# A quantized gated FFN issued from a list plan, with one elementwise step of its sigmoid on GpSimd

## The chip, the cores and the metric

The kernel runs on one core of a Trainium2 chip. The metric is the device time of one execution in microseconds; the number quoted for a kernel is the median of its runs. Five engines matter, each with its own queue, worked through in order: TensorE (PE in the profile, with PEld for its weight loads), VectorE (DVE), ScalarE (ACT), GpSimd (POOL) and SyncE (SP, which issues DMAs here). An instruction that waits for another engine holds up everything behind it in its own queue.

## The reference, cut to what matters

The reference is a two-layer decoder in float32 on x of 16 x 256 tokens with 256 features: in layer 0 a causal linear attention, a cross-attention and a mixture of experts, in layer 1 a latent attention, a second cross-attention and a gated FFN with simulated 16-bit activations. The change touches only this last FFN:

```python
def act_qdq(x):
    qmax = 2.0 ** (ACT_BITS - 1) - 1.0                      # 32767
    scale = jnp.maximum(jnp.max(jnp.abs(x)) / qmax, 1e-12)  # over the whole tensor
    return jnp.clip(jnp.round(x / scale), -qmax - 1.0, qmax) * scale
def fixed_qdq_u16(x):
    scale = 1.0 / 65536.0
    return jnp.clip(jnp.round(x / scale), 0.0, 65535.0) * scale
...
x = act_qdq(x)
up = act_qdq(x @ lpbq_dequant(w_up).T)
gate = act_qdq(x @ lpbq_dequant(w_gate).T)
sig = fixed_qdq_u16(jax.nn.sigmoid(gate))
gate = act_qdq(gate * sig)
o = act_qdq(gate * up)
return o @ lpbq_dequant(w_down).T
```

There are 4096 tokens, 256 features and 768 inner features. Each scale is a maximum over a whole tensor, so nothing can be rounded before the last element of that tensor is known. Each act_qdq is a barrier.

## The kernel before, in words

The FFN is the function l1_ffn, the last stage. Tokens lie along the free dimension in 8 groups of 512 (index n); the normalised input of a group, transposed, is F.xT[n] (tile ff_x). The 768 inner features are worked in 3 parts of 256 (index c), so that there are 24 *pieces* (n, c), each a tile of 128 partitions x 1024 floats. G[n] (ff_g) holds the gate branch of a group for the whole stage. The stage has four passes:

1. Gate. The input is rounded (rounded, L1746, on ScalarE; L1773 on VectorE) and multiplied with the gate weights; ScalarE copies each product out of PSUM (L1776), VectorE takes its peak (helper peak, L1681). Ends with scales(): a maximum over the peaks (L1732, VectorE), an all-reduce over partitions (L1734, GpSimd), a scale (L1737) and its reciprocal (L1739) on VectorE.
2. Up, first time, and the sigmoid. For each piece TensorE makes the up product, of which only the peak is kept (ff_pu). At the same time, independently of TensorE, the gate piece is rounded (ScalarE, tile ff_a), goes through the sigmoid (L1790, ScalarE, tile ff_b), is clamped to 65535/65536 and shifted by 192 (L1793), so that the low half of each float holds the 16-bit value, and is multiplied with the rounded gate (L1794, VectorE); then its peak is taken (ff_ps). Ends with two scales.
3. Up again. The same up product is made a second time, rounded straight from PSUM (ff_a), multiplied with the rounded gate (L1809) and its peak taken (ff_po). Ends with a scale.
4. Down. Each piece is rounded (L1746, L1818) and multiplied with the down weights; each output tile of 128 tokens (32 of them) is scaled and added to x (L1826) and written by a DMA from SP (L1827).

Tiles: ff_a and ff_b have three buffers each, shared by passes 2 and 3; gate and up products share three PSUM buffers (pu[...]), the output has two (po). TensorE can thus be three pieces ahead of whoever reads PSUM. A float32 matmul call appears as two matmul records. Matmuls are issued by the helper matmul_k (L422).

The order on each engine: the stages before l1_ffn run under planned(E), where E.nc is a Plan. A Plan only records calls, and Plan.issue then schedules the list: it finds what each call reads and writes, gives each a cost on its engine (class Call: VectorE 50 + 1.05 ns an element, ScalarE activation 170 + 0.73, GpSimd tensor_scalar 50 + 1.2, TensorE 0.84 twice), and picks again and again, on each engine, the call of lowest rank (place in the program) among those that could start within 150 ns of the earliest:

```python
first = min(rows)[0]
rank, index, begin, n = min(
    (r, i, b, n) for b, r, i, n in rows if b <= first + self.near
)
```

Ring objects tell the plan when a buffer of a tile ring comes free. The finished order is issued as it stands, sorted by planned start (`with self.tc.manual_schedule()`). Calls issued from a plan carry the line L322 in the profile. The FFN before is not in a plan: its calls go straight to the engines in program order and the framework's own scheduler settles each engine's order, which is why its profile lines are its own.

Of the kernel before, what the change touches and what calls it, by code (L numbers as in the profile page):

```python
# [22 lines left out]
ALU = mybir.AluOpType  # L23
AX = mybir.AxisListType
PSUM = bass.MemoryType.PSUM
# [301 lines left out]
@contextmanager  # L327
def planned(E):

    nc = E.nc  # L330
    E.nc = plan = Plan(E.tc)
    yield plan
    E.nc = nc
    plan.issue()
# [1345 lines left out]
def peak(E, out, in_, axis=AX.X):  # L1680
    E.nc.vector.tensor_reduce(out, in_, axis, ALU.max, apply_absolute_value=True)  # L1681
# [25 lines left out]
def l1_ffn(E, F):  # L1707
# [5 lines left out]

    tc, nc = E.tc, E.nc
    I16, U16 = mybir.dt.int16, mybir.dt.uint16
    MC = 2
    NP = MI // MC
    with ExitStack() as ctx:  # L1720
        c1 = ctx.enter_context(tc.tile_pool(name="ff_c", bufs=1))
        big = ctx.enter_context(tc.tile_pool(name="ff_g", bufs=1))
        wk = ctx.enter_context(tc.tile_pool(name="ff_w", bufs=3))
        pu = ctx.enter_context(tc.tile_pool(name="ff_pu", bufs=3, space=PSUM))
        po = ctx.enter_context(tc.tile_pool(name="ff_po", bufs=2, space=PSUM))
        up, gate, down = (E.ffn[n] for n in ("up", "gate", "down"))

        def scales(peaks, name, unit=None):
# [15 lines left out]
        def rounded(out, in_, inv):  # L1744

            nc.scalar.activation(out, in_, AF.Identity, bias=F.magic[:, 0:1], scale=inv[:, 0:1])  # L1746

        def low16(t, dtype):
            return t.bitcast(dtype)[:, :, ::2]
# [3 lines left out]
        def branch(w, n, c, name):  # L1753

            ps = pu.tile([P, MC, 512], F32, name="ps_" + name, tag="pu")
            for m in range(MC):
                f = slice((c * MC + m) * P, (c * MC + m + 1) * P)
                matmul_k(
                    E, ps[:, m, :], [w[:, k, f] for k in range(KD)],
                    [F.xT[n][:, k, :] for k in range(KD)],  # L1760
                )
            return ps

        def piece(n, c):
            return G[n][:, c * MC : (c + 1) * MC, :]
# [17 lines left out]
        for at, (n, c) in enumerate(pieces):  # L1783
            ps = branch(up, n, c, "up")
            peak(E, stat["u"][:, at : at + 1], ps, AX.XY)
            gp = piece(n, c)
            gq = wk.tile([P, MC, 512], F32, name="ff_a", tag="ff_a")
            rounded(gq, gp, ig)
            sig = wk.tile([P, MC, 512], F32, name="ff_b", tag="ff_b")
            nc.scalar.activation(sig, low16(gq, I16), AF.Sigmoid, scale=sg[:, 0:1])  # L1790


            nc.vector.tensor_scalar(sig, sig, 65535.0 / 65536.0, 192.0, ALU.min, ALU.add)  # L1793
            nc.vector.scalar_tensor_tensor(  # L1794
                gp, low16(gq, I16), sg16, low16(sig, U16), ALU.mult, ALU.mult
            )
            peak(E, stat["s"][:, at : at + 1], gp, AX.XY)
# [60 lines left out]
@with_exitstack  # L1858
def tile_decoder(ctx: ExitStack, tc: tile.TileContext, ins: dict, out: bass.AP):
    E = make_env(ctx, tc, ins, out)  # L1860
    with ExitStack() as outer:
        made = outer.enter_context(tc.tile_pool(name="weights_1", bufs=1))
        with ExitStack() as inner:
            W = load_weights(E, outer, inner)
            l0_attention(E, W)
            raw = load_weights_1(E, inner.enter_context(tc.tile_pool(name="raw_1", bufs=1)))
            routed, V = l0_cross(E, W, raw, made)
        with ExitStack() as inner:

            fw = ffn_weights(E, ctx, inner)  # L1870
            W.moe = inner.enter_context(tc.tile_pool(name="moe_weights", bufs=2))
            psum = inner.enter_context(tc.tile_pool(name="made_ps", bufs=1, space=PSUM))
            steps = {1: "gate", 3: "up", 5: "down"}
            l0_experts(
                E, W, routed, lambda e: fw(steps[e], psum, "pp") if e in steps else None
            )
        F = ffn_input(E, ctx)
        l1_tokens(E, W, F, V, routed)
    l1_ffn(E, F)
# [45 lines left out]
```

## Time and profile before

| what | us |
|---|---|
| median of 3 runs (1784.87 to 1789.61) | 1785.4 |
| the profiled execution | 1783.88 |
| its span, first to last instruction | 1782.1 |
| PE busy in the span | 1634.5 (92%) |
| DVE busy | 1131.0 (63%) |
| ACT busy | 697.9 (39%) |
| POOL busy | 502.9 (28%) |
| FFN: first gate matmul to the end of the span | 1422.9 to 1782.1 |

Busy times are of the whole program; they say which engine has most work, not which sets the pace of a stage. A group line of the profile reads: line, engine, operation, output<-inputs, shapes, count, then busy time in us, mean ns of one, and the idle time of the engine just before, with what ended it. A timeline line reads: start in us from the span's start, length in us, engine, line, operation. Lengths of neighbouring VectorE instructions overlap a little, so the pace of an engine is read from starts.

### The profile page before, as it was taken

How to read it: one execution, taken by the hardware profiler on the slowest of the kernel's cores; microseconds unless marked ns; L12 is line 12 of the kernel's file. 1: busy time of each engine (PE TensorE's matmuls, PEld its weight loads, DVE VectorE, ACT ScalarE, POOL GpSimd, SP SyncE). 2: the span in 40 equal slices, each digit the busy share in tenths (PEclk: the TensorE clock that was granted, in tenths of full speed). 3: DMA queues.
4: the chain of work that ended last, by engine and by line, in shares of the span. 5: the costliest groups of instructions: out<-in, count | busy, mean ns of one | idle time of the engine just before them, and what ended most of it. 6: DMA issues, size and time to landing. Idle time of an engine off the chain costs nothing.

```text
span 1782.1 us, 24580 instructions
## 1 busy us (share of the span) xinstructions
PE 1634.5 (92%) x9428; PEld 1077.5 (60%) x9428; DVE 1131.0 (63%) x2290; ACT 697.9 (39%) x1467; POOL 502.9 (28%) x547
## 2 busy tenths in 40 slices
PE   5999997999999769999997799999999599989899
PEld 3666664666666557777776466666666344434388
DVE  7867667998888633221212789876767543998751
ACT  2223222655555311111111455465556233656650
POOL 6333213455556420000001776534334100000000
PEclk9999998999999769999999899999999699999999
DMA  5000007210111133343341111000000000000011
GB/s 174 1 1 1 1 1 241 66 32 28 34 34 37 57 131 118 108 147 119 107 133 50 51 57 36 28 1 1 1 1 1 1 0 0 1 0 0 0 45 50
DMA packets 73375, 84.48 MB, mean 47 GB/s; under 512 B 11614, under 2 KB 64566, under 8 KB 73258
## 3 DMA queue, kind: packets, MB, share of 16 engines
q1 hardware_dynamic: 67114, 66.35, 11.7%
q0 software_dynamic: 6144, 16.57, 2.9%
q8 instruction: 74, 1.21, 0.3%
q14 instruction: 43, 0.35, 0.1%
HBM read 49.56 MB, written 33.56 MB: 47 GB/s over the span
## 4 chain that ended last, share of the span: by engine, by line
PE 66%; DVE 21%; issue 7%; ACT 3%; POOL 2%; DMA 1%; SPq 0%; POOLq 0%; DVEq 0%; ACTq 0%
PE ps_h L422 8%; PE ps_y L422 8%; PE ps_pr L322 7%; PE ps_av L322 7%; PE ps_sc L322 6%; PE ps_gate L422 5%; PE ps_out L422 5%; PE ps_pt L322 4%; PE ps_v L322 3%; PE ps_rec L322 3%; PE ps_po L322 3%; DVE x L322 2%; DVE ff_g L1794 2%; DVE ff_ps L1681 2%; PE ps_ht L322 1%
## 5 line engine op out<-in xcount | busy, mean ns | idle before, releaser
L1558 DVE COPY ex_y<-ps_y 128x256 f32<-128x256 f32 x80 | 34.0, 424 | 231.3 <-PE ps_y L422 231.3
L422 PE MATMUL ps_up<-ff_x,ffn_up 128*128 128x512 f32 x384 | 167.6, 595 | 10.6 <-DVE ff_pu L1681 7.8
L322 POOL DMA_INDIRECT ex_yg<-moe_y,slot x64 | 63.2, 988 | 341.6 <-DMA moe_y<-ex_y 321.2
L322 POOL TENSOR_TENSOR sa_e<-sa_e,sa_rec 128x1024 f32<-128x1024 f32 x64 | 121.4, 1904 | 118.0 <-PE ps_pt L322 62.7
L322 ACT ACTIVATE sa_e<-ps_sc,sa_top 128x256 f32<-128x256 f32 x256 | 118.4, 485 | 69.1 <-DVE sa_top L322 65.0
L422 PE MATMUL ps_h<-ex_xT,w 128*128 128x320 f32 x512 | 142.8, 437 | 0.0
L422 PE MATMUL ps_y<-w,ex_h 128*128 128x256 f32 x640 | 140.7, 379 | 0.0
L422 PEld LDWEIGHTS ps_up<-ff_x,ffn_up 128*128 128x128 f32 x384 | 72.1, 190 | 105.9 <-issue 83.0
L422 PEld LDWEIGHTS ps_y<-w,ex_h 128*128 128x128 f32 x640 | 121.6, 190 | 18.2
L1548 ACT ACTIVATE ex_h<-ps_h 128x640 f32<-128x640 f32 x64 | 45.1, 704 | 221.3 <-PE ps_h L422 221.3
L422 PEld LDWEIGHTS ps_h<-ex_xT,w 128*128 128x128 f32 x512 | 96.7, 191 | 40.0 <-issue 0.6
L322 POOL TENSOR_TENSOR lx_s<-lx_s,lx_mx 128x616 f32<-128x616 f32 x64 | 77.5, 1224 | 51.6 <-DVE lx_mx L322 35.1
L422 PE MATMUL ps_out<-ffn_down,ff_g 128*128 128x256 f32 x384 | 85.3, 386 | 7.3 <-issue 7.3
L422 PE MATMUL ps_gate<-ff_x,ffn_gate 128*128 128x512 f32 x192 | 85.4, 608 | 6.4 <-DVE ff_x L1773 6.4
L422 PEld LDWEIGHTS ps_out<-ffn_down,ff_g 128*128 128x128 f32 x384 | 74.4, 194 | 18.7 <-issue 8.1
L322 ACT COPY lx_sT<-ps_pt 77x512 f32<-77x512 f32 x117 | 65.4, 581 | 49.8 <-PE ps_pt L322 49.4
L322 DVE TENSOR_TENSOR la_at<-ps_sc,la_tri 128x1024 f32<-128x1024 f32 x64 | 76.0, 1217 | 13.9 <-PE ps_sc L322 13.9
L322 PE MATMUL ps_pt<-ident,lx_s 128*77 128x128 f32 x512 | 77.0, 285 | 6.4 <-DVE rt_hits L322 3.7
L322 DVE TENSOR_REDUCE sa_top<-ps_sc 128x4 f32<-128x1024 f32 x64 | 75.9, 1214 | 10.7 <-PE ps_sc L322 10.7
L322 PE MATMUL ps_ht<-ident,h 128*128 128x128 f32 x256 | 38.8, 293 | 42.1 <-DVE h L322 24.8
L322 PEld LDWEIGHTS ps_pt<-ident,lx_s 128*77 128x77 f32 x512 | 58.7, 150 | 25.4 <-issue 10.7
L322 POOL DMA_INDIRECT moe_x<-rh,slot x64 | 63.5, 992 | 27.7 <-issue 10.1
(295 smaller groups left out, 3419.4 us busy)
## 6 DMA issues: line engine op xcount, KB each, us to landing
w<-in_L_ffn_w SPq DMA_DIRECT2D x32, 512.0 KB, 4.4
moe_x<-rt_zero SPq DMA_DIRECT2D x16, 640.0 KB, 7.6
ex_xg<-moe_x SPq DMA_DIRECT2D x16, 640.0 KB, 6.9
moe_y<-ex_y SPq DMA_DIRECT2D x16, 640.0 KB, 5.9
x<-in_x SPq DMA_DIRECT2D x32, 128.0 KB, 3.2
out_x<-x SPq DMA_DIRECT2D x32, 128.0 KB, 1.7
w_ctx_T<-in_ctx_T SPq DMA_DIRECT2D x1, 1232.0 KB
lx_bias<-in_mask_Bx1xSxS_ff SPq DMA_DIRECT2D x8, 154.0 KB, 2.4
```

Source lines behind the costliest of these rows:

```text
L322: made = getattr(getattr(self.nc, self.engine), self.method)(*self.args, **self.kwargs)
L422: E.nc.tensor.matmul(ps, a, b, start=n == 0, stop=n == last)
L1548: nc.scalar.activation(h[:, f, :].rearrange("p (a c) -> p a c", a=2), ps[:, :, :HC], AF.Gelu)
L1558: nc.vector.tensor_copy(y[:, c, :], ps)
L1681: E.nc.vector.tensor_reduce(out, in_, axis, ALU.max, apply_absolute_value=True)
L1794: nc.vector.scalar_tensor_tensor(gp, low16(gq, I16), sg16, low16(sig, U16), ALU.mult, ALU.mult)
```

## The change

The FFN's calls are recorded in a Plan and issued from it, with Ring objects for the pools of three and two buffers, and the clamp and shift of the sigmoid goes to GpSimd in place of VectorE. The arithmetic, the tiles, their buffer counts and the number of instructions stay.

```diff
-    tc, nc = E.tc, E.nc
+    tc = E.tc
...
-    with ExitStack() as ctx:
+    with ExitStack() as ctx, planned(E) as nc:
         c1 = ctx.enter_context(tc.tile_pool(name="ff_c", bufs=1))
         big = ctx.enter_context(tc.tile_pool(name="ff_g", bufs=1))
-        wk = ctx.enter_context(tc.tile_pool(name="ff_w", bufs=3))
-        pu = ctx.enter_context(tc.tile_pool(name="ff_pu", bufs=3, space=PSUM))
-        po = ctx.enter_context(tc.tile_pool(name="ff_po", bufs=2, space=PSUM))
+        wk = nc.ring(ctx.enter_context(tc.tile_pool(name="ff_w", bufs=3)), 3)
+        pu = nc.ring(ctx.enter_context(tc.tile_pool(name="ff_pu", bufs=3, space=PSUM)), 3)
+        po = nc.ring(ctx.enter_context(tc.tile_pool(name="ff_po", bufs=2, space=PSUM)), 2)
...
-            nc.vector.tensor_scalar(sig, sig, 65535.0 / 65536.0, 192.0, ALU.min, ALU.add)
+            nc.gpsimd.tensor_scalar(sig, sig, 65535.0 / 65536.0, 192.0, ALU.min, ALU.add)
```

planned(E) puts the Plan in E.nc for the block's length and issues it at the end:

```python
@contextmanager
def planned(E):
    nc = E.nc
    E.nc = plan = Plan(E.tc)
    yield plan
    E.nc = nc
    plan.issue()
```

## The prediction

> **What bounds the stage now.** I read the page's totals first (PE busy 92%, 1634.5 of 1782.1 us), then the timeline from 1385 us to find where the FFN's passes begin and end, then busy time by stretch, the groups of the second pass, and its VectorE timeline. In the stretches the columns are PE, PEld, DVE, ACT, POOL busy, granted clock, DMA share and GB/s.
>
> ```profile
> core 0: us, PE busy (x) PEld busy (x) DVE busy (x) ACT busy (x) POOL busy (x), PEclk, DMA share, GB/s
> 1422.90:1508.10 85.20, 85.20 (x193) 37.62 (x194) 33.44 (x30) 30.14 (x30) 0.00 (x0) 0.97 0.00 0
> ...
> 1517.00:1611.20 94.20, 86.32 (x196) 36.12 (x194) 93.86 (x95) 52.60 (x45) 0.01 (x1) 1.00 0.00 1
> 1611.20:1686.30 75.10, 72.39 (x169) 31.84 (x168) 56.10 (x53) 54.14 (x47) 0.69 (x2) 1.00 0.00 0
> 1686.30:1693.60 7.30, 0.00 (x0) 0.01 (x1) 5.17 (x9) 3.26 (x3) 0.35 (x1) 0.83 0.00 0
> 1693.60:1782.10 88.50, 85.29 (x384) 74.35 (x384) 30.55 (x55) 25.24 (x23) 0.00 (x0) 0.98 0.14 48
> ```
>
> Passes 1 (gate), 3 (second up) and 4 (down) are TensorE's: it has no idle time in them but at their edges. Pass 2 is VectorE's: 93.86 of 94.20 us busy. Its groups (busy us, mean ns of one, idle before) and a stretch of its timeline (start, us):
>
> ```profile
> L1794 DVE SCALAR_TENSOR_TENSOR ff_g<-ff_a,ff_sg,ff_b 128x1024 f32<-128x1024 int16 x24 | 30.4, 1272 | 0.0
> L1681 DVE TENSOR_REDUCE ff_pu<-ps_up 128x1 f32<-128x1024 f32 x24 | 29.1, 1213 | 2.3 <-PE ps_up L422 2.2
> L1681 DVE TENSOR_REDUCE ff_ps<-ff_g 128x1 f32<-128x1024 f32 x24 | 28.9, 1206 | 0.0
> L1793 DVE TENSOR_SCALAR ff_b<-ff_b 128x1024 f32<-128x1024 f32 x24 | 16.3, 681 | 0.5 <-ACT ff_b L1790 0.5
> ```
>
> ```profile
> 1568.07 1.21 DVE L1681 TENSOR_REDUCE ff_ps<-ff_g 128x1 f32<-128x1024 f32 x1
> 1569.19 1.27 DVE L1794 SCALAR_TENSOR_TENSOR ff_g<-ff_a,ff_sg,ff_b 128x1024 f32<-128x1024 int16 x1
> 1570.39 1.21 DVE L1681 TENSOR_REDUCE ff_pu<-ps_up 128x1 f32<-128x1024 f32 x1
> 1571.52 1.20 DVE L1681 TENSOR_REDUCE ff_ps<-ff_g 128x1 f32<-128x1024 f32 x1
> 1572.65 0.68 DVE L1793 TENSOR_SCALAR ff_b<-ff_b 128x1024 f32<-128x1024 f32 x1
> 1573.25 1.21 DVE L1681 TENSOR_REDUCE ff_pu<-ps_up 128x1 f32<-128x1024 f32 x1
> 1574.38 1.27 DVE L1794 SCALAR_TENSOR_TENSOR ff_g<-ff_a,ff_sg,ff_b 128x1024 f32<-128x1024 int16 x1
> 1575.57 0.68 DVE L1793 TENSOR_SCALAR ff_b<-ff_b 128x1024 f32<-128x1024 f32 x1
> 1576.18 1.20 DVE L1681 TENSOR_REDUCE ff_ps<-ff_g 128x1 f32<-128x1024 f32 x1
> ```
>
> The pattern repeats after two pieces, 1568.07 to 1576.18: 8.11 us, 4.055 a piece. Starts count, not durations: the two peaks (u: maximum of the up product; s: of the gated one) each take 1.13, the product (L1794, "STT" below) 1.19 and the clamp 0.60, since neighbours overlap by 0.08. TensorE needs 8 matmuls at 0.429, 3.43 a piece, and waits: 8 waits on the u peak, 7.8 us, then 2.7 us on the first rounding of pass 3.
>
> [...] The STT reads two SBUF tiles, the clamp on GpSimd reads SBUF[...] (timelines of POOL and DVE):
>
> ```profile
> 1105.65 3.77 POOL L322 TENSOR_TENSOR sa_e<-sa_e,sa_rec 128x1024 f32<-128x1024 f32 x2
> 1106.59 3.65 DVE L322 SCALAR_TENSOR_TENSOR x<-ex_yg,wgt,x 128x256 f32<-128x256 f32 x2
> 1114.43 0.47 DVE L322 SCALAR_TENSOR_TENSOR x<-ex_yg,wgt,x 128x256 f32<-128x256 f32 x1
> ```
>
> Such an STT takes 0.47 alone; two behind a GpSimd pair that ends at 1109.42 last until 1110.24. In the other order (STT first at 1125.76, GpSimd at 1125.98) the GpSimd one lengthened only from 1.90 to 1.98. [...] The nearest row:
>
> ```profile
> L322 POOL TENSOR_SCALAR la_z<-la_q,hh_odd 128x512 f32<-128x512 f32 x16 | 11.1, 696 | 0.0
> ```
>
> **The change, part by part.** (a) 24 clamps leave VectorE: 24 x 0.60 = 14.4 us. GpSimd, otherwise empty here, gets them. Twice the width of that row bounds one from above at 1.39; taking off one fixed 0.1 (the smallest memsets of this trace) gives 1.29 at 128x1024. I take 1.3. Had it 2.0 a piece, it would still fit the cycle below, so this price alone decides nothing.
>
> (b) The order. I followed the planner's rules (lowest rank within 150 ns of the earliest start). TensorE, ScalarE, GpSimd and SP keep in essence today's order; the output DMAs still follow their tiles. On VectorE it is u peak, STT, s peak of one piece, then of the next. So each s peak stands right behind the STT whose result it reads. Pass 3 shows what such a pair costs: product at 1687.60 (1.23 long), its peak at 1688.86, the previous one's end plus 0.03, where independent neighbours overlap by 0.08. I take 1.27 + 0.04 = 1.31 for STT to s peak, in place of 1.19. A piece is then 1.31 + 1.13 + 1.13 = 3.57 us, still above TensorE's 3.43: **VectorE stays the bound of pass 2**, though barely. With 1.19 it would be 3.45.
>
> (c) The new wait, STT behind clamp. Take E, the end of piece k-3's STT. The rings of three make ScalarE start piece k there: rounding at E+0.04 (1559.43 to 1559.47 in the trace), sigmoid 1.27 later, 1.147 long, so clamp k reaches GpSimd at about E+2.54 (0.08 to hand over, as after ln_var). VectorE does s peak and u peak in between and starts the STT of k-2 at E+0.04+2.26 = E+2.30. The STT is first by 0.24 us, the clamp waits, runs until 1.3 after the STT's end, and is done 1.0 before the next STT. So in the steady state the wait falls on GpSimd and costs nothing; cover: 2.3 us of peaks against 1.3 of clamp.
>
> (d) The start. Scale known at 1511.65; rounding, table load and sigmoid end the first ScalarE chain at 1516.53 as now; clamp 0 runs 1516.6 to 1517.9. Clamp 1, whose sigmoid ended at 1517.57, follows at once [...] so STT 0, today at 1518.21, runs 1519.2 to 1520.5. Peak u1, today done before STT 0, now stands behind it in the queue. STT 1 starts at 1520.5+0.04+2.26 = 1522.8.
>
> (e) The end. STT 23 starts at 1522.8+22x3.57 = 1601.3, the last s peak ends at 1603.9 (today 1612.27). The order puts the u maximum behind that peak, where today it stands ahead of it: maximum, all-reduce, scale, reciprocal and rounding then take about 2.3 after the peak (today 1.6), and TensorE goes on with piece 4 of pass 3 at **1606.2, today at 1613.90: 7.7 us earlier**. Its three pieces ahead are done by 1604.9, so it idles some 1.3 there; 0.14 a piece in pass 2.
>
> (f) The rest costs nothing in my sum. Pass 1 and pass 3 are covered by TensorE (ScalarE and VectorE need about 2.4 us of its 3.43). The 7.3 us from pass 3 to 4 are one chain of data, which no order shortens. The start of pass 4 at half speed remains (slowest matmul 763 ns against 379)[...]. The plan lets TensorE begin a second output tile while waiting for rounded pieces; those come each 1.13, faster than the slow matmuls use them. The first all-reduce after elementwise work stood still 1.1 us (input ready 1418.78, start 1419.92), the others 0.1; if this recurs after the clamps, it costs 0 to 2.2. I take 0, as it was the first of its kind.
>
> **Sum.** The profiled run took 1783.9 (span 1782.1 and 1.8 around it), 1.5 under the median of 1785.4. 1783.9 - 7.7 = 1776.2; against the median, 1777.7. I say **1778**.
>
> **Rivals.** *TensorE becomes the bound (faster still)*: if STT to s peak costs 1.19 and start and contention are free, pass 2 runs at TensorE's pace. All 48 up pieces take 48x3.43 = 164.6 from 1508.08, today 178.2 (to 1686.27): 13.6 less, 1772. Half of it (period 3.45, my start) gives 10.6, 1775. For: the margin is 0.1 a piece; against: the pairs in pass 3.
> *The clamp wins the race (slower)*: if it starts ahead of the STT each time, the STT waits from E+2.30 to E+3.84: 1.54 x 22 = 34 lost, 26 slower than now, 1812. For: only 0.24 us part them, and the trace's GpSimd work does hold VectorE up. Against: each link of that 0.24 is measured, and the order re-forms at each STT. The turning point is a mean wait of 7.7/22 = 0.35 a piece; a race lost every other time gives 1795.
> *No visible effect*: the wait averages 0.15 to 0.35, or the all-reduce delay recurs; 1780 to 1786.
>
> **How the numbers follow.** About 0.3%, 5.4 us, is what a measurement here can tell from no change. Forecast, with its small costs, 0.45; TensorE bound or half of it 0.18; no visible effect 0.17; the race lost, wholly or half, 0.20. Faster 0.63, same 0.17, slower 0.20. Range 1770 to 1796: it leaves out the fully lost race and a little beneath.
>
> **What would show it.** STT group still near 1.27 us mean, the clamp group longer than 1.3 (about 2.3, with its waiting); VectorE starts per piece 3.57; the first STT record near 2.5 us; TensorE's resumption near 1606; passes 1, 3, 4 as long as now. A mean STT above 1.6 means the race is being lost, and I am wrong.

## The result, and the profile after

| | before | after |
|---|---|---|
| median, us (16 runs each) | 1785.1 (1783.4 to 1789.6) | 1789.3 (1788.0 to 1792.4) |
| the profiled execution, us | 1783.9 | 1790.0 |
| its span, us | 1782.1 | 1787.9 |
| mean granted TensorE clock | 0.958 | 0.952 |

The ratio after to before is 1.0023 [1.0016, 1.0031]: 4.2 us slower, where 7 us faster was forecast. The time is inside the range; the direction is wrong.

The two profiles do not reach the FFN at the same time: the first gate matmul stands at 1422.89 before and at 1424.80 after. The code ahead of it is the same, and that start varies by some us between profiles of other kernels below too. So every run is read from its own first gate matmul, in three legs: to the resumption of TensorE in pass 3 (the matmul that waited for the first rounding), from there to the first down matmul, and from there to the end of the span. The table also holds the experiments told below; it is worked out from each timeline of TensorE.

| kernel | gate to resumption | to first down matmul | to the end | FFN |
|---|---|---|---|---|
| before | 191.01 | 79.72 | 88.5 | 359.2 |
| after | 192.56 | 82.35 | 88.2 | 363.1 |
| e1, plan alone | 198.17 | 80.93 | 89.4 | 368.5 |
| e2, GpSimd alone | 193.36 | 82.33 | 88.8 | 364.4 |
| e3, a cheap pair of operations | 184.24 | 82.34 | 88.5 | 355.1 |
| e6, four clamps back on VectorE | 185.43 | 80.93 | 89.0 | 355.4 |
| e7, e1 with the s peak later | 191.72 | 82.16 | 88.5 | 362.4 |
| e8, e6 with the s peak later | 184.25 | 83.54 | 88.3 | 356.1 |
| e9, e6 without the plan | 184.86 | 79.71 | 88.4 | 353.0 |
| e10, e6 with four buffers for ff_b | 185.58 | 80.82 | 89.1 | 355.5 |

The FFN after is 3.9 us longer, close to the difference of the medians (4.2); the other 1.9 of the spans' difference lies ahead of it. The forecast had the first leg at 1606.2 - 1422.9 = 183.3. It is 192.6.

The tile view of ff_b (ns: minimum, median, maximum; first and last start) says why at once:

```profile
L322 POOL TENSOR_SCALAR ff_b<-ff_b x24: 3624/3624/3667, 1520.5 to 1605.7; 128x1024 f32<-128x1024 f32 x24
L322 DVE SCALAR_TENSOR_TENSOR ff_g<-ff_a,ff_sg,ff_b x24: 1276/1402/2159, 1524.2 to 1610.1; 128x1024 f32<-128x1024 int16 x24
```

A clamp on GpSimd takes 3.62 us, not 1.3. The minimum equals the median, so this is not waiting for VectorE's product: it is the work itself (e4 below finds about the same price with no product beside it). With 0.08 between neighbours, GpSimd needs 3.70 a piece and has become the bound of pass 2. Its timeline (start, length; in brackets idle time before, and what ended it):

```profile
1512.78 0.35 POOL L322 PARTITION_ALL_REDUCE ff_sg<-ff_mg  x1 [90.58 <-DVE ff_mg L322]
1520.47 88.86 POOL L322 TENSOR_SCALAR ff_b<-ff_b 128x1024 f32<-128x1024 f32 x24 [7.34 <-PE ps_up L322]
1615.24 0.38 POOL L322 PARTITION_ALL_REDUCE ff_su<-ff_mu  x1 [5.92 <-issue]
```

All 24 clamps stand in one unbroken row. On both sides of it GpSimd does nothing: 7.34 us after the all-reduce, 5.92 us before the next. The release named for the first, PE ps_up, is work that a clamp does not read; its sigmoid was ready about 2 us earlier. VectorE at the same two places:

```profile
1513.63 1.23 DVE L322 TENSOR_REDUCE ff_pu<-ps_up 128x1 f32<-128x1024 f32 x1
1524.17 2.16 DVE L322 SCALAR_TENSOR_TENSOR ff_g<-ff_a,ff_sg,ff_b 128x1024 f32<-128x1024 int16 x1 [9.31 <-POOL ff_b L322]
1526.37 1.22 DVE L322 TENSOR_REDUCE ff_ps<-ff_g 128x1 f32<-128x1024 f32 x1
1527.50 1.22 DVE L322 TENSOR_REDUCE ff_pu<-ps_up 128x1 f32<-128x1024 f32 x1
1528.63 1.40 DVE L322 SCALAR_TENSOR_TENSOR ff_g<-ff_a,ff_sg,ff_b 128x1024 f32<-128x1024 int16 x1
1530.07 1.22 DVE L322 TENSOR_REDUCE ff_ps<-ff_g 128x1 f32<-128x1024 f32 x1
```

The planned order is the predicted one: product, s peak, u peak. But the first product waits 9.31 us for its clamp. Behind it in the queue stands the u peak of the second piece, whose up product was made by 1516.9 (16 of the 32 matmuls that TensorE runs from 1510.00 to 1523.90): the peak starts at 1527.50, and TensorE waits 4.88 us for it. Later products last 1.40 in place of 1.28, so that VectorE goes at GpSimd's 3.70. These products do not wait for their own clamps, which are done 0.8 earlier. Beside each runs the clamp of the next piece; for the product at 1528.63 it is this one:

```profile
1527.92 3.62 POOL L322 TENSOR_SCALAR ff_b<-ff_b 128x1024 f32<-128x1024 f32 x1
```

The product starts 0.71 us after this clamp and ends at 1530.03, 1.5 before it. What holds it is taken up under e6 and in the section on the prediction. TensorE (first line of pass 3 that waited, and the start of pass 4):

```profile
1617.36 74.06 PE L322 MATMUL ps_up<-ff_x,ffn_up 128*128 128x512 f32 x168 [3.40 <-ACT ff_a L322]
1699.71 30.53 PE L322 MATMUL ps_out<-ffn_down,ff_g 128*128 128x256 f32 x132 [8.29 <-issue]
```

The same two places before, where the 168 matmuls took 72.37 after a wait of 2.67, and the wait ahead of pass 4 was 7.35:

```profile
1613.90 72.37 PE L422 MATMUL ps_up<-ff_x,ffn_up 128*128 128x512 f32 x168 [2.67 <-ACT ff_a L1746]
1693.62 85.29 PE L422 MATMUL ps_out<-ffn_down,ff_g 128*128 128x256 f32 x384 [7.35 <-issue]
```

### The profile page after: what moved, and what is told of

It is laid out like the page before. It is cut to its first block, busy times and chain, and to the rows that moved or that the text cites. A ratio compares the mean times of both kernels' runs of the same rounds, so it can differ in the third digit from the quotient of the medians.

```text
span 1787.9 us, 24631 instructions
## 1 busy us (share of the span) xinstructions
PE 1642.7 (92%) x9428; PEld 1079.5 (60%) x9428; DVE 1122.4 (63%) x2266; ACT 698.6 (39%) x1467; POOL 589.1 (33%) x571
## 4 chain that ended last, share of the span: by engine, by line
PE 65%; DVE 22%; issue 8%; ACT 2%; POOL 2%; DMA 1%; SPq 0%; POOLq 0%; DVEq 0%; ACTq 0%
PE ps_h L422 8%; PE ps_y L422 8%; PE ps_pr L322 7%; PE ps_av L322 7%; PE ps_sc L322 6%; PE ps_gate L322 5%; PE ps_out L322 5%; PE ps_pt L322 4%; PE ps_v L322 3%; PE ps_rec L322 3%; PE ps_po L322 3%; DVE x L322 2%; DVE ff_g L322 2%; DVE ff_ps L322 2%; DVE ff_pu L322 1%
## 5 line engine op out<-in xcount | busy, mean ns | idle before, releaser
L322 PE MATMUL ps_up<-ff_x,ffn_up 128*128 128x512 f32 x384 | 173.1, 607 | 8.3 <-DVE ff_pu L322 4.9
L322 POOL TENSOR_SCALAR ff_b<-ff_b 128x1024 f32<-128x1024 f32 x24 | 87.0, 3626 | 9.2 <-PE ps_up L322 7.3
L322 DVE TENSOR_REDUCE sa_top<-ps_sc 128x4 f32<-128x1024 f32 x64 | 76.0, 1215 | 10.7 <-PE ps_sc L322 10.7
L322 POOL TENSOR_TENSOR ln_rstd<-ln_var,neghalf 128x4 f32<-128x4 f32 x40 | 41.0, 1026 | 101.2 <-DVE ln_var L322 100.9
```

The costliest lines, as they stand in the source:

```text
L322: made = getattr(getattr(self.nc, self.engine), self.method)(*self.args, **self.kwargs)
```

## The experiments

My theory after the result: three terms of the sum were wrong. The clamp costs 3.62 because of its pair of operations; GpSimd pays some 6 to 7 us whenever it changes between all-reduce and elementwise work, and about 2 of it is uncovered on each side; and the plan's order costs what step (b) said. Rivals: it is GpSimd itself that is slow on this shape whatever the operation; the clamps wait for VectorE; the plan's order alone is the loss. Ratios are to the kernel before on the same chip.

**e1, the plan alone.**

```diff
-            nc.gpsimd.tensor_scalar(sig, sig, 65535.0 / 65536.0, 192.0, ALU.min, ALU.add)
+            nc.vector.tensor_scalar(sig, sig, 65535.0 / 65536.0, 192.0, ALU.min, ALU.add)
```

> The FFN issued from the plan, the clamp left on VectorE. Order theory (the plan's order itself costs): VectorE goes u peak, clamp, product, s peak for one piece, so two pairs of each piece stand directly behind the instruction whose result they read: 1.13 + 0.72 + 1.31 + 1.13 = 4.29 us a piece where before has 4.055; 24 pieces are 5.6 us, so about 1791 us. GpSimd theory (all of the loss comes from the clamp's place): the plan is neutral, 1785 us, 4.05 a piece.

1794.1 us, ratio 1.0047 [1.0031, 1.0064]. VectorE's timeline:

```profile
1561.42 0.68 DVE L322 TENSOR_SCALAR ff_b<-ff_b 128x1024 f32<-128x1024 f32 x1
1562.14 1.28 DVE L322 SCALAR_TENSOR_TENSOR ff_g<-ff_a,ff_sg,ff_b 128x1024 f32<-128x1024 int16 x1
1563.46 1.22 DVE L322 TENSOR_REDUCE ff_ps<-ff_g 128x1 f32<-128x1024 f32 x1
1564.60 1.22 DVE L322 TENSOR_REDUCE ff_pu<-ps_up 128x1 f32<-128x1024 f32 x1
1565.73 0.69 DVE L322 TENSOR_SCALAR ff_b<-ff_b 128x1024 f32<-128x1024 f32 x1
```

The plan puts the clamp, the product that reads it and the peak that reads the product in a row. Clamp to product is 0.72 where it was 0.60, product to s peak 1.32 where it was 1.19: 4.31 a piece against 4.055. The pace is the expected one, the time 3 us above the expected 1791: of the 9.3 us that the FFN is longer, 7.2 lie in the first leg, 1.2 in the second and 0.9 in pass 4. The plan without the move to GpSimd is a loss of 9 us.

**e2, GpSimd alone.** The FFN outside a plan, as before, with only this line changed:

```diff
-            nc.vector.tensor_scalar(sig, sig, 65535.0 / 65536.0, 192.0, ALU.min, ALU.add)
+            nc.gpsimd.tensor_scalar(sig, sig, 65535.0 / 65536.0, 192.0, ALU.min, ALU.add)
```

> The clamp on GpSimd, no plan. GpSimd theory (a clamp costs 3.62 us there and sets the pace, and the first clamp and the all-reduce behind the clamps each stand still for 2 to 2.5 us): as slow as the changed kernel or within 2 us of it, 1787 to 1790 us, 3.7 us a piece. Order theory: without the plan's order the forecast's gain appears, 1776 to 1781 us.

1791.5 us, ratio 1.0039 [1.0024, 1.0053]. The timeline of GpSimd shows the same price and the same two standstills, without any plan:

```profile
1521.74 11.08 POOL L1793 TENSOR_SCALAR ff_b<-ff_b 128x1024 f32<-128x1024 f32 x3 [6.94 <-ACT ff_b L1790]
1533.70 78.65 POOL L1793 TENSOR_SCALAR ff_b<-ff_b 128x1024 f32<-128x1024 f32 x21 [0.89 <-ACT ff_b L1790]
1618.40 0.38 POOL L1734 PARTITION_ALL_REDUCE ff_su<-ff_mu  x1 [6.05 <-issue]
```

So neither belongs to the plan. Each half of the change loses, 9 and 6 us; both together lose 4. They overlap: with the clamp gone, VectorE's own 3.57 lies under GpSimd's 3.70, and the longer pairs of the plan's order no longer set the pace.

**e3, another pair of operations on the same tile, engine and queue.** The clamp and shift are replaced by two multiplications by one, so the values behind the sigmoid are others.

```diff
-            nc.gpsimd.tensor_scalar(sig, sig, 65535.0 / 65536.0, 192.0, ALU.min, ALU.add)
+            nc.gpsimd.tensor_scalar(sig, sig, 1.0, 1.0, ALU.mult, ALU.mult)
```

> The changed kernel with the GpSimd instruction's operations and constants replaced: times 1.0, times 1.0, in place of minimum and add, so the 16-bit value of the sigmoid isn't formed (that part of the computation is changed); tiles, places and waits are the same. Price theory (minimum and add in this form are what is slow on GpSimd): the group falls from 3.62 to about 1.3 us, the product from 1.40 to 1.27, the pace to 3.57 on VectorE, and the time to about 1782 us, since the two standstills of GpSimd stay. Contention theory (the instruction is slow [...] because of its size): the group stays near 3.6 us and the time near 1789.

1781.7 us, ratio 0.9982 [0.9975, 0.9989], as the price theory had it (1782). So it is not GpSimd as such that is slow on this shape. The tile view and the timelines of GpSimd and VectorE:

```profile
L322 POOL TENSOR_SCALAR ff_b<-ff_b x24: 1037/1886/2007, 1520.8 to 1598.1; 128x1024 f32<-128x1024 f32 x24
L322 DVE SCALAR_TENSOR_TENSOR ff_g<-ff_a,ff_sg,ff_b x24: 1274/1276/2058, 1521.9 to 1605.0; 128x1024 f32<-128x1024 int16 x24
```

```profile
1520.84 4.04 POOL L322 TENSOR_SCALAR ff_b<-ff_b 128x1024 f32<-128x1024 f32 x3 [7.26 <-ACT ff_b L322]
1526.58 1.89 POOL L322 TENSOR_SCALAR ff_b<-ff_b 128x1024 f32<-128x1024 f32 x1 [1.69 <-ACT ff_b L322]
1530.15 1.89 POOL L322 TENSOR_SCALAR ff_b<-ff_b 128x1024 f32<-128x1024 f32 x1 [1.69 <-ACT ff_b L322]
...
1607.74 0.38 POOL L322 PARTITION_ALL_REDUCE ff_su<-ff_mu  x1 [7.72 <-DVE ff_ms L322]
```

```profile
1526.28 1.28 DVE L322 SCALAR_TENSOR_TENSOR ff_g<-ff_a,ff_sg,ff_b 128x1024 f32<-128x1024 int16 x1
1527.59 1.22 DVE L322 TENSOR_REDUCE ff_ps<-ff_g 128x1 f32<-128x1024 f32 x1
1528.73 1.21 DVE L322 TENSOR_REDUCE ff_pu<-ps_up 128x1 f32<-128x1024 f32 x1
1529.86 1.27 DVE L322 SCALAR_TENSOR_TENSOR ff_g<-ff_a,ff_sg,ff_b 128x1024 f32<-128x1024 int16 x1
```

This is nearly the predicted steady state: product first (1526.28), GpSimd 0.30 later (1526.58), its 1.04 of work stretched to 1.89, so that it ends 0.91 after the product, VectorE at 3.57 to 3.58. The 7.26 us ahead of the first one are still there; the all-reduce at the end is not late, against my expectation, since the last elementwise instruction ended 7.72 us before, long enough to cover the standstill.

**e4 and e5, prices.** Outside a plan and with the clamp on VectorE, a row of instructions on a scratch tile that nothing else reads, in pass 1, where GpSimd is otherwise empty:

```diff
         sx, ix = scales(F.peaks, "x")
+        pt = c1.tile([P, 1024], F32, name="ff_pt")
+        ...
+        nc.gpsimd.tensor_scalar(pt, pt, 65535.0 / 65536.0, 192.0, ALU.min, ALU.add)
+        nc.gpsimd.tensor_scalar(pt, pt, 1.0, 1.0, ALU.mult, ALU.mult)
+        ...
```

> The kernel before with eleven further GpSimd instructions on a scratch tile, issued one behind the other during pass 1, where VectorE runs no two-input instruction: minimum and add, multiply twice (constants, then with a pointer scalar), minimum alone, add alone, multiply and add, add and minimum, minimum with a pointer scalar, the first again at half width, maximum and add. Price theory: those with minimum or maximum take about 3.6 us at 1024 elements and about 1.85 at 512, those with multiply and add alone 1.3. Contention theory: all take about 1.3, as nothing competes. Either way the all-reduce at the end of pass 1 stands still for about 2.5 us, if changing from elementwise work to an all-reduce is what costs it.

> The kernel before with further GpSimd instructions on a scratch tile in pass 1, 128x1024 each. The first price list had 1.04 us for multiply-multiply and multiply-add, 2.8 for minimum or add alone, 3.6 for pairs that begin with minimum, maximum or add. If a leading multiply is what makes the form fast: multiply-minimum and multiply-subtract 1.04, all pairs that begin with another operation 3.6. If it is that both operations are among multiply and add: add-multiply and add-add 1.04 too, multiply-minimum slow at 2.8 to 3.6. The first elementwise instruction behind the all-reduce starts about 7.3 us after the all-reduce's end whatever its inputs do, if changing the kind of work is the cost.

One timed run each, 1783.5 and 1783.7: the row hides in pass 1. Five lines of e4's timeline of GpSimd: the first elementwise instruction behind an all-reduce; min then add; two multiplications; min alone; multiplication then addition.

```profile
1427.29 0.18 POOL L1774 TENSOR_SCALAR ff_pk<-ff_sx 128x1 f32<-128x1 f32 x1 [7.30 <-DVE ff_x L1788]
...
1429.18 3.96 POOL L1776 TENSOR_SCALAR ff_pt<-ff_pt 128x1024 f32<-128x1024 f32 x1
1433.23 1.04 POOL L1777 TENSOR_SCALAR ff_pt<-ff_pt 128x1024 f32<-128x1024 f32 x1
...
1435.57 2.78 POOL L1779 TENSOR_SCALAR ff_pt<-ff_pt 128x1024 f32<-128x1024 f32 x1
...
1441.31 1.04 POOL L1781 TENSOR_SCALAR ff_pt<-ff_pt 128x1024 f32<-128x1024 f32 x1
```

The prices of both with constants, at 128x1024 in float32:

| pair in one GpSimd instruction | us |
|---|---|
| multiply, multiply; multiply, add; add, multiply; a copy | 1.04 |
| one operation alone: min, add or multiply | 2.78 to 2.79 |
| add, min; min, multiply; max, add; max, min; add, add; multiply, subtract | 3.63 to 3.65 |
| min, add; multiply, min (each the first slow one of its row; in the changed kernel min, add is 3.62) | 3.96 |

At half the width min, add took 1.92; with one constant read from a tile in place of an immediate, multiply, multiply took 1.12 and min, add 3.71. VectorE runs no product here, so the price is not a wait for it. None of the forms that I expected is right. The speed does not follow from min or max being there (add, add is slow, and so is a lone multiplication), nor from a leading multiplication (multiply, min is slow, add, multiply is not), nor from both operations being among multiply and add (add, add again). The runs show three cheap pairs, about 2.7 times their price for a single operation and about 3.5 times for the other pairs; why, they do not show.

The first line also tests the change-over. This instruction reads only the input's scale, which VectorE had ready at 1420.18, and yet starts at 1427.29, 7.30 us after the all-reduce (7.05 in e5); the release named, DVE ff_x, is work that it does not read. So that standstill is no wait for an input.

**e6, both change-overs covered.** Pieces 0, 1, 22 and 23 keep their clamp on VectorE, 20 pieces stay on GpSimd, in the plan.

```diff
-            nc.gpsimd.tensor_scalar(sig, sig, 65535.0 / 65536.0, 192.0, ALU.min, ALU.add)
+            clamp = nc.vector if at in (0, 1, 22, 23) else nc.gpsimd
+            clamp.tensor_scalar(sig, sig, 65535.0 / 65536.0, 192.0, ALU.min, ALU.add)
```

> The changed kernel with the clamps of pieces 0, 1, 22 and 23 on VectorE and the other 20 on GpSimd. Change-over theory (GpSimd needs 7.3 us from an all-reduce to elementwise work and 5.9 us back, and both lay on the path): the first product comes as early as before, the two all-reduces at the end follow their inputs at once, TensorE's gap before pass 3 falls under 2 us and it resumes at full speed; the pace stays 3.70 in between. About 1780 us. If the price alone were the cause: 1786 to 1788, since 20 of 24 clamps still cost 3.62.

1781.1 us, ratio 0.9979 [0.9972, 0.9986]. GpSimd's timeline:

```profile
1522.20 74.08 POOL L322 TENSOR_SCALAR ff_b<-ff_b 128x1024 f32<-128x1024 f32 x20 [8.77 <-ACT ff_b L322]
1608.43 0.38 POOL L322 PARTITION_ALL_REDUCE ff_su<-ff_mu  x1 [12.15 <-DVE ff_ms L322]
```

The price per clamp is the same, and 7.7 us of the FFN's length are gone against the changed kernel. They are gone at the edges: from the first product to the end of the last s peak it is 88.7, against 88.5. The first product comes 5.0 earlier after the first gate matmul, 2.0 by the change-over and 3.0 because its clamp takes 0.7 on VectorE; the end, from the last s peak to the resumption, is 2.3 in place of 4.7. The clamps on GpSimd end 12 us before the all-reduce, which now comes as soon as its input is there, and TensorE resumes after 1.75 us of idleness without loss (72.37 for the 168 matmuls, as in before). This version, with the change's own arithmetic, is 4 us faster than the kernel before, 0.2%.

It also shows when a clamp holds a product up. In the first GpSimd pieces VectorE goes at 3.57 and each product falls 0.12 closer to the start of the clamp beside it. One early and one late pair of clamp and product (single lines of the two timelines):

```profile
1540.78 3.63 POOL L322 TENSOR_SCALAR ff_b<-ff_b 128x1024 f32<-128x1024 f32 x1
1541.73 1.28 DVE L322 SCALAR_TENSOR_TENSOR ff_g<-ff_a,ff_sg,ff_b 128x1024 f32<-128x1024 int16 x1
...
1548.19 3.62 POOL L322 TENSOR_SCALAR ff_b<-ff_b 128x1024 f32<-128x1024 f32 x1
1548.90 1.40 DVE L322 SCALAR_TENSOR_TENSOR ff_g<-ff_a,ff_sg,ff_b 128x1024 f32<-128x1024 int16 x1
```

Started 0.95 us into the clamp, the product is not held at all; started 0.71 into it, it lasts 0.12 longer, and there the two engines stay locked at 3.70. In all six kernels with this clamp on GpSimd (after, e2, e6, e8, e9, e10), the products that start up to 0.83 us into a clamp end 2.11 to 2.13 after its start, mostly 1.40 or 1.52 long; those that start later keep 1.27 to 1.29. That is as if the clamp held them for its first 0.84 us and they then took their usual 1.27.

**e7, e1 with the s peak one piece later.** If e1's loss is the order of dependent neighbours, parting product and peak in the program must give it back. The edit also puts the s peak between a clamp and the product that reads it.

```diff
+            late()
             nc.vector.scalar_tensor_tensor(
                 gp, low16(gq, I16), sg16, low16(sig, U16), ALU.mult, ALU.mult
             )
-            peak(E, stat["s"][:, at : at + 1], gp, AX.XY)
+            def late(at=at, gp=gp):
+                peak(E, stat["s"][:, at : at + 1], gp, AX.XY)
         su, iu = scales(stat["u"], "u")
+        late()
```

> The plan with the clamp on VectorE (as in the plan-only run), but the s peak of each piece recorded one piece later, so that no VectorE instruction stands directly behind the one whose result it reads, save the first. Order theory: pace 4.05 us in place of 4.30, time about 1786 to 1787, 6 to 8 less than plan-only. If the distance between product and peak doesn't matter: 4.30 and 1794 as in plan-only.

1788.6 us, ratio 1.0020 [1.0012, 1.0029], 5.5 us under e1 and 2 above what was expected. VectorE's timeline:

```profile
1560.19 0.68 DVE L322 TENSOR_SCALAR ff_b<-ff_b 128x1024 f32<-128x1024 f32 x1
1560.79 1.21 DVE L322 TENSOR_REDUCE ff_ps<-ff_g 128x1 f32<-128x1024 f32 x1
1561.92 1.27 DVE L322 SCALAR_TENSOR_TENSOR ff_g<-ff_a,ff_sg,ff_b 128x1024 f32<-128x1024 int16 x1
1563.11 1.22 DVE L322 TENSOR_REDUCE ff_pu<-ps_up 128x1 f32<-128x1024 f32 x1
1564.24 0.68 DVE L322 TENSOR_SCALAR ff_b<-ff_b 128x1024 f32<-128x1024 f32 x1
```

The same four instructions, in an order in which none reads the result of its neighbour, take 4.05 a piece, the pace of the kernel before; the starts are 0.60, 1.13, 1.19 and 1.13 apart. What e7 still loses against before lies mostly in the second leg (82.16 against 79.72: 1.7 by slower matmuls, 0.7 by a longer gap ahead of pass 4).

**e8, e6 with the s peak later.** The same edit on e6.

> The edges kernel with the s peak one piece later too. Change-over and price theory: in the middle of pass 2 GpSimd sets the pace at 3.70, so nothing changes there; at the edges, where VectorE sets it, four pieces gain 0.25 each and the u maximum comes one peak earlier: 1778 to 1780. If VectorE were the bound in the middle, 20 x 0.12 = 2.4 more: 1776.

1781.6 us, ratio 0.9980 [0.9973, 0.9987]: no better than e6, where 1778 to 1780 was expected. In pass 2 GpSimd's 3.70 is the bound in either order. The first leg is 1.2 shorter, and the second gives it back, 2.6 longer, 2.1 of it in the gap ahead of pass 4 (10.68 against 8.56).

**e9, e6 outside the plan**, and **e10, e6 with a fourth buffer for ff_b alone**, for that second leg, which is longer in all planned kernels. e9 is the kernel before with e6's two lines for the clamp. The edit of e10:

```diff
         wk = nc.ring(ctx.enter_context(tc.tile_pool(name="ff_w", bufs=3)), 3)
+        wb = nc.ring(ctx.enter_context(tc.tile_pool(name="ff_wb", bufs=4)), 4)
...
-            sig = wk.tile([P, MC, 512], F32, name="ff_b", tag="ff_b")
+            sig = wb.tile([P, MC, 512], F32, name="ff_b", tag="ff_b")
...
-            gq = wk.tile([P, MC, 512], F32, name="ff_b", tag="ff_b")
+            gq = wb.tile([P, MC, 512], F32, name="ff_b", tag="ff_b")
```

> The FFN as before, outside a plan; the clamps of pieces 0, 1, 22, 23 stay on VectorE, those of pieces 2 to 21 go to GpSimd with min and add unchanged (3.62 us each). This takes the plan out of the variant in which both change-overs of GpSimd are hidden (1781.1). Theory (the plan's order is the cause of the longer way from pass 3 to pass 4): the gap before pass 4 is back at 7.35 us as in the kernel before (8.56 in the planned variant), and so the time is about 1 us under the planned variant, 1779 to 1781, if GpSimd's 3.62 us a piece, not the order of the peaks, sets pass 2's pace of about 3.7 in both. Rival (the plan gains in pass 2 what it loses there, because outside it the tail of pass 2 is ordered less well): the first rounding of pass 3 comes 1 us or more later than in the planned variant, and the time is 1781 to 1784. Both change-overs hidden, so no wait of 5.9 us ahead of the all-reduce in either theory.

> The planned variant with hidden change-overs (clamps of pieces 0, 1, 22, 23 on VectorE), with four buffers in place of three for the tile ff_b alone. Theory (in pass 3 the plan puts the rounding of ff_b, which waits for the product three pieces back, ahead of the rounding of the up product on ScalarE; a fourth buffer takes that wait away): pass 3 runs without VectorE falling behind, the gap from pass 3 to pass 4 is 7.3 to 7.5 us in place of 8.56, and the time is 1779.5 to 1780.5. Rival (the longer gap is the order of the last products and peaks on VectorE itself): the gap stays at 8.5 or more and the time within 0.5 us of 1781. In pass 2 the fourth buffer lets sigmoids run a piece further ahead; GpSimd is the pace there, so 3.62 to 3.70 a piece in both.

On the chip that ran these two, all three kernels were slower, before at 1804.9 (the first gate matmul stands at 1446.23 in e9 and 1444.22 in e10, some 20 later than in the other kernels, so the difference lies ahead of the FFN); the ratios count: e9 0.9967 [0.9955, 0.9979], e10 0.9974 [0.9963, 0.9985]. The waits of TensorE ahead of pass 4, e9 first, e10 second (total us, times, longest):

```profile
PE ps_out L422 <- issue: 7.3, 1, 7.3
```

```profile
PE ps_out L322 <- issue: 8.5, 1, 8.5
```

Without the plan the gap is the old 7.35 and the second leg the old 79.7, with the same clamps on the same engines: the longer gap belongs to the plan's order. The fourth buffer does not shorten it: the theory of e10 falls. ScalarE still waits for a product before 14 of its 24 roundings of ff_b (17.1 us in all). That chain (rounding of ff_b, rounding of ff_a, product) goes round in about 3.6 us a piece in e9 as well, so it alone does not part the two. The timelines do show where the time goes. In before and e9 the last product starts as soon as the last up product is rounded (0.03 and 0.04 us after). In the planned kernels VectorE is then still at the products before it, and the last one starts 0.98 late in after, 1.25 in e6 and 1.22 in e10, about what their gaps are longer (0.9, 1.2 and 1.1). Which of the plan's choices puts VectorE behind there stays open. By ratio e9 is the best version run; its interval overlaps those of e6 and e10, so only the gap is shown, not the rank.

## Why the prediction was wrong

The first leg came out 9.25 us longer than forecast (192.56 against 183.3), and the parts can be read off, all measured from the first gate matmul:

- **Step (d), the start.** The first product begins 3.1 later than written. The first clamp starts 2.0 late, behind the change-over. The rest, 1.1, is the clamp's price: 3.62 in place of two clamps of 1.3, ahead of the first product.
- **Step (a), the price.** From the first product to the end of the last s peak it is 88.5, not 84.7. Of the 3.8, 22 pieces at 3.70 in place of 3.57 are 3.0, the first product's own stretch of 0.9 the rest.
- **Step (e), the end.** From the last s peak to the resumption it is 4.7, not 2.3: the all-reduce starts 2.5 us after its input is ready (1615.24 against 1612.73), where 0.1 is usual.

Two more terms are of the second leg and together +2.6: 1.7 for a slow restart of TensorE, 0.9 for the longer gap to pass 4, which (f) put at nothing. Forecast -7.7, +9.25, +2.6, -0.3 in pass 4: 3.9 us, as found.

By size, the price makes up about 5.0 of the first leg's 9.25 (1.1, 3.0 and the 0.9 of the first product, which runs beside a clamp), the two change-overs 4.4.

**The step that failed first is the price in (a).** I took 1.3, called 1.29 to 1.39 its bounds, and wrote that it decides nothing; it measured 3.62. The bounds came from a row of the same instruction and type that multiplies twice (L531 of the kernel), not from a min and an add. For two multiplications they would have served (1.04 in e3 and e4); for another pair of operations such a row bounds nothing. At 1.04 (e3) the cycle of (c) holds, at 3.62 GpSimd is the bound, and no cover of 2.3 us of peaks was wide enough. Against VectorE's 0.68 for the clamp, GpSimd takes 1.5 times as long with a cheap pair (1.04) and 5.3 times with the clamp itself (3.62).

**The second is the change-over.** (f) put its return behind the clamps at nothing, and did not have the other direction. A timeline of the kernel before had it, in the first all-reduce and the elementwise instruction ahead of it:

```profile
1412.99 1.01 POOL L322 TENSOR_TENSOR ln_rstd<-ln_var,neghalf 128x4 f32<-128x4 f32 x1 [17.40 <-DVE ln_var L322]
1419.92 0.38 POOL L1734 PARTITION_ALL_REDUCE ff_sx<-ff_mx  x1 [5.92 <-issue]
```

I measured from its input, got 1.1 us of standstill, and took it for a thing of the first call. Measured from GpSimd's last elementwise work it is 5.9, and so it is at the end of the clamps in the changed kernel (5.92) and in e2 (6.05). In the other direction it is 7.3 (after, e3, e4) and 6.9 to 7.1 (e2, e5). Where these spans have passed before the next input comes (e3 at the end, e6 and e9 on both sides), nothing is lost; in the changed kernel 2.0 and 2.4 are. The end's part hangs on the price: at 1.04 (e3) GpSimd is done early enough. So it is no thing of the first call: in these runs it is back wherever the next input was there in time, at 5.8 to 6.1 us in one direction and 6.9 to 7.3 in the other. What GpSimd does meanwhile they do not show.

**The restart.** In the changed kernel and in e2, where TensorE stood 3.4 and 4.8 us, the 168 matmuls of pass 3 took 74.06 and 74.98; in before, e6 and e9, after 1.75 to 2.7, they took 72.37. The granted clock over the first 3.4 us of pass 3 was 0.60 in the changed kernel and 1.00 in before. I expected a slow start for pass 4 alone (a clock of 0.50 over its first 3.4 us in both kernels, behind 7.35 and 8.29 us of standstill), since with a resumption at 1606 the idle time here was to be 1.3. The length of the idle time is not the whole of it: e7 lost the same 1.7 behind a wait of only 2.03 (resumption at 1614.70; a clock of 0.51 from 1616 to 1618 and of 0.64 from 1618 to 1620), and before lost nothing behind 2.67. So it is a risk at such a pause, and no threshold is shown here.

**What was right.** The plan's order and, for a cheap pair of operations, VectorE as the bound of pass 2, (b): 1.31 for a product and its own peak, 3.57 a piece (e3 1.31 and 3.57 to 3.58; e1 1.32; undone in e7). The race of (c), in e3: the product is first by 0.30 (written 0.24), the wait falls on GpSimd, 1.04 stretched to 1.89. The 7.7 us that were forecast are also nearly there to be had: e3's first leg is 184.2 against 183.3. (f) said that no order shortens the way from pass 3 to 4; an order can lengthen it, by 0.7 to 3.3 us in the planned kernels (waits of 8.1 to 10.7 against 7.35).

**What was half right is the rule of the race.** In (c) and (d) I took it that of clamp and product the one that starts second waits until the other has ended, and that the peaks are not held. For this pair it was my assumption: before the result only products behind two other GpSimd instructions showed it (those from 1105.65 and 1106.59). The peaks bear it out: beside the clamps their medians are 1.215 us (u) and 1.220 (s), against 1.213 and 1.206 before. Where the product is first, the traces are near it: in e3 the clamp takes 0.85 longer with 0.98 of the product still to run, and in e2 one that starts 0.22 after a product takes 4.54 in place of 3.63, 0.91 longer with 1.05 to run. Where the slow clamp is first they do not bear it out: it holds the product for about its first 0.84 us, not for 3.62 (the lines under e6). The first product of the changed kernel, whose record starts 0.05 ahead of a clamp's, was held as well (2.16 in place of 1.28), so records this close do not tell who is first.

Of the rivals, the half of "no visible effect" in which the all-reduce delay recurs came true; its companion, the mean wait of a product, is 0.13 (1.40 against 1.27). The race was lost in the order of starts, by 0.71 at each piece of the changed kernel, but this costs 0.13 a piece and not the 1.54 of that rival. The slower side was reached by a mechanism that I had not listed, GpSimd as the bound; the turning point was near in my own text, "Had it 2.0 a piece, it would still fit the cycle below", and needed only the question what happens at 3.6. That 1789 lies in my range is luck: the range's slow side was drawn for a race half lost.

## What to carry to other kernels

A price taken from a row of the profile must be of the same operation, not only of the same instruction, engine and type; if there is none, say from which price on the moved work becomes the bound, and give that case its chance. An engine that alternates between two kinds of work can pay for each change (GpSimd here 5.9 us one way and 7.3 the other), so measure its standstill from its own last work, not from the arrival of the input, and leave the edges of a stage to another engine. A list order that is right in rank can still put an instruction right behind the one whose result it reads, and on a bounding engine that is paid for every piece (0.25 us in e1).

## What the runs showed of the hardware

GpSimd's tensor_scalar on 128x1024 float32 takes 1.04 us for multiply-multiply, multiply-add and add-multiply, 2.8 for a single operation, and 3.6 for the other pairs tried (up to 4.0 for the first of a row; all in e4 and e5). One multiplication alone (2.79) is dearer than two (1.04). Its change between all-reduce and elementwise work costs 5.8 to 6.1 us from elementwise to all-reduce and 6.9 to 7.3 back, counted from GpSimd's last work, wherever inputs were ready before. A clamp of 3.62 on GpSimd holds up a VectorE product of ff_a and ff_b only for about its first 0.84 us, by the ends of the products, 2.11 to 2.13 after the clamp's start. On VectorE an instruction of this size that reads its neighbour's result starts 0.12 to 0.13 later than one that does not (e1 against before: 0.72 and 1.32 behind its neighbour's start, against 0.60 and 1.19).
